# Maxima chunks of an attention step at four places instead of two

## The chip, the cores and the metric

The kernel runs on one core of a Trainium2 chip. The metric is the device time of one launch in microseconds. Matrix products run on TensorE (PE in the profile, its weight loads PEld), reductions and elementwise work on VectorE (DVE), exponentials and copies out of the accumulators on ScalarE (ACT), a few small operations on GpSimd (POOL). SyncE (SP) issues most of the DMAs.

## What is computed

The input is x (16 batches of 256 tokens with 128 channels) and a context of 1601 tokens with 64 channels per batch. Four layers follow each other, each one an attention over the context and a feed-forward part, with residuals and layer norms. What matters here is the attention over the context, with 16 heads. In layers l0, l1 and l3 a head has 8 channels, in l2 it has 32:

```python
scores = jnp.einsum('bhqd,bhkd->bhqk', qh, kh) * scale      # 256 queries x 1601 keys
attn = jax.nn.softmax(scores, axis=-1)
out = jnp.einsum('bhqk,bhkd->bhqd', attn, vh)
```

l0 and l2 have a second attention of x to itself (256 keys), the "own attention" below. Keys, values and feed-forward parts need further matrix products.

## The kernel before

**Slabs and steps.** The attention over the context of one batch and one layer is cut into four slabs of four heads each: 16 batches x 4 layers x 4 = 256 slabs, one after the other. The keys of a head lie on 32 partitions, so the four heads of a slab lie on the four 32-row strips of TensorE. A slab has seven steps (`Slab.steps`, L530): six over two tiles of 128 keys, and a last one over the remaining 65 keys. The scores of a step are transposed: keys on partitions, queries along the free dimension. `st_ops` (L447) computes eight score products (twice as many instructions for l2, whose keys are plain float32) and adds the negated maximum of each query with four further matmuls, the "shift" (st<-nmT,ones). `exps` (L462) takes the exponential on ScalarE, twice per step. `weigh` (L473) multiplies the probabilities with the values into the accumulator `av`, one step later: the values of step j-1 follow the scores of step j (`weigh_back`, L1132).

**Maxima.** The shift of a slab must be known before its first step. It is made during the slab before: `Slab.maxima` (L544) pops one chunk, a matmul of 128 queries of one head with some 400 keys into one bank of the accumulators (bank<-k,q), and a reduction to the maximum on VectorE (mx<-bank, L552). A slab has 2 x 4 x 4 = 32 chunks; the head changes fastest, so neighbouring chunks lie on different strips. When all 32 are done, `Slab.thirds` (L556) reduces them to one negated maximum per query and head (nm, L558) and splits it on POOL into three bfloat16 parts with four operations (L509 to L512); `Slab.shift` (L561) transposes them on TensorE (bank<-ident,nmp) and ScalarE copies the result (nmT).

**Banks.** The pool `pb` (L156) has four banks. They serve the chunks, the accumulator `av` of the slab (held for all its steps), and the products of all other work. The pool `ps` has two buffers for scores, of two banks each.

**Slots.** All other work (layer norms, feed-forward parts, keys, values, own attention, the end of a slab) is written as generators. `slot` (L1073) advances each of them by one piece: first what waits in `later` (the end of a slab, `finish`, L1115), then the line of the keys or of the values in turn, then the chains of the two batches in work and the loading of contexts. A slot can emit much work on TensorE or none. Each step has two slots at its end.

**Order.** The order of the instructions on each engine is the order in which the program emits them; a wait holds up what comes behind it on the same engine. In a step before the change it is: chunks up to `part - 3` (L1173), scores and exponentials (L1176, L1177), three chunks (L1179), values of the step before (L1180), two slots. `part` runs 5, 10, 16, 21, 26, 32, so a step has two or three chunks ahead of the scores and three behind them. `maxima` (L1157) emits the matmuls of one place first and their reductions after them. The last step has no chunks: it begins with `thirds`, and `shift` stands between the values and the slots.

Of the kernel before, what the change touches and what calls it, by code (L numbers as in the profile page):

```python
# [54 lines left out]
def rows_of(kt):  # L55
    return min(P, NK - kt * P)
# [18 lines left out]
def model(ctx: ExitStack, tc: tile.TileContext, d, out):  # L75
# [88 lines left out]
    def bank():  # L164
        return pb.tile([P, 512], F32, tag="bank", name=name("bank"))
# [5 lines left out]
    def mm(o, l, r, start=True, stop=True, free=False):  # L171
        nc.tensor.matmul(out=o, lhsT=l, rhs=r, start=start, stop=stop, skip_group_check=free)  # L172
# [274 lines left out]
    def st_ops(att, s, t0, n, r, nmT, pairs=(0, 1)):  # L447


        sc = {hp: ps.tile([P, 2, 2, T], F32, tag="st", name=name("st")) for hp in pairs}  # L450
        heads = [g for hp in pairs for g in (2 * hp, 2 * hp + 1)]
        for i in range(n):
            k0 = (t0 + i) * P
            for g in heads:
                h = slice(32 * g, 32 * g + 32)
                mm(sc[g // 2][:r, g % 2, i, :], att.k[s][h, k0 : k0 + r], att.q[h, s, :], i == 0, False)
        for g in heads:
            h = slice(32 * g, 32 * g + 32)
            mm(sc[g // 2][:r, g % 2, :n, :], ones16[h, :r], nmT[h, :].unsqueeze(1).broadcast_to([32, n, T]), False, True)
        return [sc[hp] for hp in pairs]  # L460

    def exps(att, sc, n, r):  # L462
        e = probs()
        nc.scalar.activation(e[:r, :, :n, :], sc[:r, :, :n, :], AF.Exp, scale=att.scale)  # L464
        return e

    def zeroed(att):
        a = bank().rearrange("p (u q) -> p u q", u=2)
        n = 1 if att.d8 else 2
        mm(a[:, :n, :], zero16[:, :P], zero16.unsqueeze(1).broadcast_to([1, n, T]), True, False, True)  # L470
        return a

    def weigh(att, s, av, pr, t0, n, r, last, heads=range(4), sums=True, values=True):  # L473
        for i in range(n):
            fin = last and i == n - 1
            if values:
                for g in heads:
                    m = 9 if att.d8 else 32
                    mm(av[32 * g : 32 * g + m, 0, :], att.value(s, t0 + i, g, r), pr[g // 2][:r, g % 2, i, :],
                       False, fin, True)  # L480
            if sums and not att.d8:
                for g in heads:
                    mm(av[32 * g : 32 * g + 32, 1, :], ones[:r, :32], pr[g // 2][:r, g % 2, i, :], False, fin, True)
# [43 lines left out]
    class Slab:  # L527


        steps = [(t, min(2, NT - t), rows_of(t)) for t in range(0, NT, 2)]  # L530
# [13 lines left out]
        def maxima(self):  # L544

            g, q, c, k0, k1 = self.todo.popleft()
            att, s = self.att, self.s
            p = bank()
            h = slice(32 * g, 32 * g + 32)

            def reduce():
                nc.vector.tensor_reduce(self.mx[:, q, g, c : c + 1], p[:, : k1 - k0], AX.X, ALU.max)  # L552

            return lambda: mm(p[:, : k1 - k0], att.q[h, s, q * P : (q + 1) * P], att.k[s][h, k0:k1]), reduce
# [501 lines left out]
    def advance(g):  # L1056
        try:
            return True, next(g)
        except StopIteration:
            return False, None  # L1060

    def begin():

        while began[0] < nb:
            b = began[0]
            n = None if b < LANES else seq.index((b - LANES, "l3"))
            if n is not None and not (n in k_done and n in v_done):
                return
            chains.append([None, load_ctx(b)])
            chains.append([b, life(b)])  # L1070
            began[0] += 1

    def slot():  # L1073
        begin()
        if later:
            g = later.popleft()
            if advance(g)[0]:
                later.appendleft(g)
        for i, l in enumerate(lines):
            if i == turn[0] % 2:  # L1080
                advance(l)
        turn[0] += 1
        for c in list(chains):
            if c[0] is not None and c[0] in ready:
                if not ready[c[0]].done:
                    continue
                del ready[c[0]]
            alive, att = advance(c[1])
            if att is not None:
                ready[c[0]] = att  # L1090
            if not alive:
                chains.remove(c)

    def until(cond):
        for _ in range(2000):
            if cond():
                return
            slot()
        raise RuntimeError("the slots do not come to an end")
# [3 lines left out]
    def slab(i):  # L1103

        n, s = divmod(i, 4)
        if n >= len(seq):
            return None
        b = seq[n][0]
        until(lambda: b in ready and not ready[b].done and n in k_of and s in k_of[n])
        att = ready[b]  # L1110
        att.k, att.v = k_of[n], v_of.setdefault(n, {})
        slabs_of[i] = Slab(att, s, i % 2)
        return slabs_of[i]

    def finish(sl, i):  # L1115

        yield from normalised(sl.att, sl.s, sl.av)
        if sl.s == 3:
            sl.att.done = True
        if not sl.att.d8 or sl.s == 3:  # L1120
            vp_room.give()

    with tc.manual_schedule():
        sl = slab(0)
        while sl.todo:
            for o in sl.maxima():
                o()
        sl.thirds()
        sl.shift()
        back = None  # L1130

        def weigh_back():  # L1132

            nonlocal back
            if back is None:
                return
            sl, i, j, pr = back
            n = i // 4
            t0, m, r = sl.steps[j]
            if j == 0:  # L1140
                until(lambda: (0 if sl.att.d8 else sl.s) in v_of.get(n, {}))
                sl.att.v = v_of[n]
                sl.av = zeroed(sl.att)
            last = j == len(sl.steps) - 1
            weigh(sl.att, sl.s, sl.av, pr, t0, m, r, last)
            back = None
            if last:
                g = finish(sl, i)
                if advance(g)[0]:
                    later.append(g)  # L1150

        for i in range(4 * len(seq)):
            nxt = slab(i + 1)
            steps = sl.steps
            emitted = 0

            def maxima(want):  # L1157

                nonlocal emitted
                ops = []  # L1160
                while nxt is not None and emitted < want:
                    a, c = nxt.maxima()
                    a()
                    ops.append(c)
                    emitted += 1
                for c in ops:
                    c()

            for j, (t0, m, r) in enumerate(steps):

                part = 32 * (j + 1) // (len(steps) - 1)
                if j < len(steps) - 1:
                    maxima(part - 3)  # L1173
                elif nxt is not None:
                    nxt.thirds()
                sc = st_ops(sl.att, sl.s, t0, m, r, sl.nmT)  # L1176
                pr = [exps(sl.att, t, m, r) for t in sc]  # L1177
                if j < len(steps) - 1:
                    maxima(part)  # L1179
                weigh_back()  # L1180
                back = (sl, i, j, pr)
                if j == len(steps) - 1 and nxt is not None:
                    nxt.shift()
                slot()
                slot()
            kp_room.give()
            sl = nxt
        weigh_back()
        until(lambda: not chains and not later)
# [119 lines left out]
```

## Time and profile before

| what | value |
|---|---|
| time, median of 3 runs | 11254.35 us (11251.69 to 11277.46) |
| the profiled execution | 11315.87 us, span 11313.9 us |
| mean granted clock of TensorE | 0.795 |
| ScalarE, exponentials (L464) | 3840, 3500.6 us busy |
| TensorE, values (bank<-p,v) | 2483.3 us busy |
| TensorE, scores (st<-q,k) | 2011.0 us busy |
| TensorE, shift (st<-nmT,ones) | 1291.8 us busy |
| VectorE, nm of a slab (L558) | 256, 186 ns each in the middle |
| DMA, mean busy share of the queue q1 | 11.4% |

A group in the profile is named by the source line of the instruction, its engine and operation, and "what it writes <- what it reads". Nearly all matmuls have the line of one helper, L172, so they are told apart by their tiles. Busy time counts overlapping matmuls of one group once. "Granted clock" is the share of the full clock that TensorE was given in a stretch. A row of the timeline gives start, length, engine, line, operation and tiles, how many instructions are merged in it, and in brackets how long the engine was idle before and for whom it waited.

### The profile page before, as it was taken

The numbers are of one execution on the slowest core, as the hardware profiler recorded it, in microseconds if no ns is written. First come the engines' busy times: TensorE is split into PE (matmuls) and PEld (weight loads), VectorE is DVE, ScalarE is ACT, GpSimd is POOL, SyncE is SP. The second block draws the span as 40 slices with busy tenths as digits, with TensorE's granted clock in tenths as the row PEclk, the third lists the DMA queues.
The fourth block names the chain that finished last, engine by engine and source line by source line (L and its number), as shares of the span: only waits on it lengthen the run. The fifth ranks groups of instructions, "written<-read, shape, count | busy, mean of one in ns | idle before, by whom it ended". The sixth has DMA issues, their size and how long they took to land.

```text
span 11313.9 us, 204909 instructions
## 1 busy us (share of the span) xinstructions
PE 9940.3 (88%) x86834; PEld 5384.7 (48%) x86874; DVE 5942.1 (53%) x13070; ACT 4978.6 (44%) x6812; POOL 952.6 (8%) x2283
## 2 busy tenths in 40 slices
PE   6989899898998979989798897988989989798898
PEld 3445444454444544445454454544544445454454
DVE  4544555445554455545555454554555545455455
ACT  3433454334543445434454344543444434444344
POOL 2000100001000010000100001000010000100000
PEclk7679777796777977789777896778977689777897
DMA  2100111001110011100111001110011100111011
GB/s 57 36 7 15 35 44 36 7 18 36 40 36 7 18 38 39 36 7 18 42 39 31 7 19 42 37 31 7 20 43 36 31 7 19 43 36 32 7 23 26
DMA packets 158827, 313.09 MB, mean 28 GB/s; under 512 B 65163, under 2 KB 116275, under 8 KB 157910
## 3 DMA queue, kind: packets, MB, share of 16 engines
q1 hardware_dynamic: 154676, 297.83, 11.4%
q8 instruction: 683, 11.19, 0.4%
q14 instruction: 234, 1.92, 0.1%
q0 software_dynamic: 768, 1.48, 0.0%
q10 hardware_dynamic: 2466, 0.68, 0.0%
HBM read 98.31 MB, written 2.10 MB: 9 GB/s over the span
## 4 chain that ended last, share of the span: by engine, by line
PE 73%; DVE 13%; ACT 5%; issue 4%; POOL 3%; SPq 2%; DMA 1%; DVEq 0%; POOLq 0%; ACTq 0%
PE bank L172 58%; PE st L172 10%; DVE mx L552 4%; ACT p L464 3%; DVE nm L579 2%; SPq L411 2%; PE mx L172 1%; PE bank L492 1%; PE bank L298 1%; POOL rs L278 1%; DVE z L282 1%; POOL p L603 1%; DVE st L275 1%; DVE hl L405 1%; ACT y L239 1%
## 5 line engine op out<-in xcount | busy, mean ns | idle before, releaser
L552 DVE TENSOR_REDUCE mx<-bank 128x1 f32<-128x400 f32 (+2 forms) x8192 | 4165.5, 568 | 2382.7 <-PE bank L172 2292.8
L464 ACT ACTIVATE p<-st 128x1024 f32<-128x1024 f32 (+1 forms) x3840 | 3500.6, 963 | 3735.0 <-PE st L172 2376.3
L172 PE MATMUL bank<-k,q 32*128 32x400 f32 (+2 forms) x10240 | 3663.6, 574 | 479.6 <-DVE mx L552 265.8
L172 PEld LDWEIGHTS bank<-k,q 32*128 32x128 f32 x10240 | 1653.0, 216 | 1900.6 <-DVE mx L552 1065.7
L172 PE MATMUL bank<-p,v 128*9 128x256 f32 (+3 forms) x27648 | 2483.3, 472 | 32.5 <-POOL p L603 32.5
L172 PE MATMUL st<-q,k 32*128 32x256 f32 (+1 forms) x18176 | 2011.0, 394 | 156.5 <-DVE nm L579 82.4
L172 PEld LDWEIGHTS st<-q,k 32*128 32x128 f32 (+1 forms) x18176 | 1313.4, 213 | 507.4 <-ACT p L464 174.3
L172 PE MATMUL st<-nmT,ones 32*128 32x512 bf16 (+1 forms) x7680 | 1291.8, 442 | 0.0
L172 PEld LDWEIGHTS bank<-p,v 128*9 128x9 f32 (+3 forms) x27648 | 688.0, 105 | 1243.6 <-issue 988.7
L172 PE MATMUL bank<-p,ones 128*32 128x256 f32 (+1 forms) x7680 | 611.3, 392 | 20.2 <-ACT p L464 20.2
L509 POOL CAST nmp<-nm 128x8 bf16<-128x8 f32 x384 | 83.7, 218 | 6017.6 <-DVE nm L558 4434.6
L579 DVE TENSOR_REDUCE nm<-mx 128x4 f32<-128x1024 f32 x256 | 301.7, 1221 | 317.2 <-PE mx L172 312.5
L172 PEld LDWEIGHTS <-ones 32*128 32x128 bf16 (+1 forms) x7680 | 410.2, 109 | 41.1
L278 POOL TENSOR_TENSOR rs<-rs,neghalf 128x2 f32<-128x2 f32 x240 | 167.6, 698 | 3002.5 <-DVE rs L277 3002.5
L239 ACT COPY v<-bank 128x512 f32<-128x512 f32 (+3 forms) x592 | 228.8, 449 | 372.2 <-PE bank L172 372.2
L172 PEld LDWEIGHTS bank<-p,ones 128*32 128x32 f32 (+1 forms) x7680 | 251.8, 113 | 217.2 <-ACT p L464 39.4
L603 POOL TENSOR_SCALAR_AFFINE_SELECT p<-p 128x1024 f32<-128x1024 f32 x256 | 266.6, 1063 | 841.6 <-PE bank L172 524.1
L502 DVE RECIPROCAL rc<-bank 128x256 f32<-128x256 f32 x128 | 224.7, 1756 | 175.4 <-PE bank L172 171.6
L172 PE MATMUL bank<-ws,h 128*128 128x128 f32 x1664 | 307.0, 351 | 3.2 <-DVE h L1027 0.8
L464 ACT ACT_TABLE_LOAD x141 | 180.9, 1283 | 262.0 <-PE st L172 139.1
L172 PEld LDWEIGHTS bank<-ws,h 128*128 128x128 f32 x1664 | 275.7, 255 | 38.6 <-DVE h L1027 12.5
L492 PE MATMUL bank<-ident,y 128*128 128x128 f32 x512 | 136.3, 360 | 155.1 <-ACT y L239 154.6
(240 smaller groups left out, 7258.1 us busy)
## 6 DMA issues: line engine op xcount, KB each, us to landing
k<-hl SPq DMA_DIRECT2D x768, 200.2 KB, 4.0
q<-hl SPq DMA_DIRECT2D x1024, 32.0 KB, 1.9
ws<-in_s_l_a_li_dram SPq DMA_DIRECT2D x32, 768.0 KB, 4.2
ws<-in_s_l3f_dram SPq DMA_DIRECT2D x32, 768.0 KB, 6.7
ws<-in_s_l0f_dram SPq DMA_DIRECT2D x32, 512.0 KB, 5.5
ws<-in_s_l_a_qkv_dram SPq DMA_DIRECT2D x16, 768.0 KB
k<-hl SPq DMA_DIRECT2D x256, 32.0 KB, 1.9
ws<-in_s_l3f_dram SPq DMA_DIRECT2D x16, 384.0 KB
```

What stands on the lines that cost most here:

```text
L172: nc.tensor.matmul(out=o, lhsT=l, rhs=r, start=start, stop=stop, skip_group_check=free)
L239: nc.scalar.copy(o, i)
L275: nc.vector.bn_stats(out=st[:, q, :], in_=src[:, q, :])
L278: nc.gpsimd.tensor_tensor(rs, rs, neghalf[:, 0:2], ALU.pow)
L282: nc.vector.tensor_scalar(z[:, q, :], src[:, q, :], mv[:, q, 0:1], rs[:, q : q + 1], ALU.subtract, ALU.mult)
L411: nc.sync.dma_start(out=raw(o)[r::4, :], in_=raw(hl[c])[32 * s : 32 * s + 32, :])
L464: nc.scalar.activation(e[:r, :, :n, :], sc[:r, :, :n, :], AF.Exp, scale=att.scale)
L492: nc.tensor.transpose(t[:, q * P : (q + 1) * P], y[:, q * P : (q + 1) * P], ident)
L502: nc.vector.reciprocal(rc, av[:, 1, :])
L552: nc.vector.tensor_reduce(self.mx[:, q, g, c : c + 1], p[:, : k1 - k0], AX.X, ALU.max)
L579: nc.vector.tensor_reduce(o, sc[hp], AX.X, ALU.max, negate=True)
L603: nc.gpsimd.affine_select(out=e, in_=e, pattern=[[0, 2], [sign * P, 2], [-sign, T]], compare_op=op, fill=0.0, base=0, channel_multiplier=sign,
```

## The change

The chunks of a step stand at four places instead of two: ahead of the scores, behind the exponentials, behind the values of the step before, and between the two slots. `ends` holds how many chunks of the 32 are to be out at each place; over the six steps with chunks it runs 1, 2, 4, 5 | 6, 8, 9, 10 | 12, 13, 14, 16 | 17, 18, 20, 21 | 22, 24, 25, 26 | 28, 29, 30, 32. So each place has one or two chunks, and a step has five or six as before. In the last step all ends are 0 and no chunk is emitted; `thirds` and `shift` stand where they stood.

```diff
-                part = 32 * (j + 1) // (len(steps) - 1)
-                if j < len(steps) - 1:
-                    maxima(part - 3)
-                elif nxt is not None:
-                    nxt.thirds()
+
+                ends = [32 * (4 * j + k) // (4 * (len(steps) - 1)) for k in range(1, 5)]
+                if j == len(steps) - 1:
+                    ends = [0] * 4
+                    if nxt is not None:
+                        nxt.thirds()
+                maxima(ends[0])
                 sc = st_ops(sl.att, sl.s, t0, m, r, sl.nmT)
                 pr = [exps(sl.att, t, m, r) for t in sc]
-                if j < len(steps) - 1:
-                    maxima(part)
+                maxima(ends[1])
                 weigh_back()
                 back = (sl, i, j, pr)
                 if j == len(steps) - 1 and nxt is not None:
                     nxt.shift()
+                maxima(ends[2])
                 slot()
+                maxima(ends[3])
                 slot()
```

## The prediction

> **What bounds the kernel now.** I read the page first (shares, clock, chain, groups), then the totals of the waits, then the timeline of single steps, then a table by stretches.
>
> ```profile
> PE 9940.3 (88%) x86834; PEld 5384.7 (48%) x86874; DVE 5942.1 (53%) x13070; ACT 4978.6 (44%) x6812; POOL 952.6 (8%) x2283
> ...
> PE 73%; DVE 13%; ACT 5%; issue 4%; POOL 3%; SPq 2%; DMA 1%; DVEq 0%; POOLq 0%; ACTq 0%
> ...
> L552 DVE TENSOR_REDUCE mx<-bank 128x1 f32<-128x400 f32 (+2 forms) x8192 | 4165.5, 568 | 2382.7 <-PE bank L172 2292.8
> ...
> L172 PE MATMUL bank<-k,q 32*128 32x400 f32 (+2 forms) x10240 | 3663.6, 574 | 479.6 <-DVE mx L552 265.8
> ```
>
> TensorE bounds: busy 88% of the span, 73% of the chain, at a mean granted clock of 0.795. The chunks of the maxima (bank<-k,q) alone have it busy for 3663.6 us, beside or without other work. There are 8192 of them, 32 for each of 256 slabs, each with one reduction on VectorE; the 64 slabs of layer l2, with plain f32 keys, need two matmul instructions per chunk (6144 + 2 x 2048 = 10240).
>
> ```profile
> PEld bank L172 <- DVE mx L552: 1282.9, 3016, 5.7
> ...
> PE bank L172 <- DVE mx L552: 265.8, 316, 5.4
> ...
> PE bank L492 <- ACT y L239: 154.6, 201, 2.4
> ```
>
> These are waits: who waited for whom, us in total, how often, longest. A chunk's weight load waits 3016 times for a reduction: it wants one of the four banks, and one is held by av for the whole slab. The wait costs more than TensorE's own 265.8 us of idleness, because chunks that wait come one by one. A step with 8-wide heads shows it:
>
> ```profile
> 3016.14 0.45 PE L172 MATMUL bank<-k,q 32*128 32x402 f32 x2
> ...
> 3016.73 1.45 PE L172 MATMUL bank<-k,q 32*128 32x402 f32 x3
> ...
> 3018.11 1.05 PE L172 MATMUL bank<-p,v 128*9 128x256 f32 x16
> ...
> 3020.15 0.45 PE L172 MATMUL bank<-k,q 32*128 32x400 f32 x2
> ```
>
> Two chunks before the scores start together and run beside them: they use other 32-row strips. Of the three after the scores, the first still fits beside the shift matmuls; the other two wait for banks and stand alone, some 0.48 us each. First chunk to values: 1.97 us.
>
> ```profile
> 3180.47:3185.28 4.81, 4.81 (x40) 2.28 (x36) 2.98 (x6) 1.94 (x2) 0.00 (x0) 0.50 0.00 0
> 3188.48:3191.43 2.95, 2.91 (x37) 1.51 (x33) 2.50 (x6) 2.16 (x3) 0.00 (x0) 1.00 0.00 0
> ```
>
> Two steps whose slots are empty (length, then busy PE, PEld, DVE, ACT, POOL, clock): 4.81 us at clock 0.50 and 2.95 us at 1.00. In the second VectorE is near its limit, 2.50 us for 5 reductions, 0.50 each in a row; it idles 0.45 us while the values run.
>
> [...]
>
> **The change part by part.** Nothing is removed or added in kind: 8192 chunks, 8192 reductions, same operands, no DMA. [...] Now the ends run 1, 2, 4, 5, 6, 8, 9, 10, 12 and so on: four places with 1 or 2, 5.33 per step in both. I went through the matmuls in order of time and counted what stands between two groups of values. Of 869 full 8-wide steps 31% have no slot work on TensorE, 28% up to 1.5 us (I take it as one slot working), 41% more (both); of those with none 44% run at full clock. There are 1152 such steps with chunks and 384 of l2.
>
> *The block around the scores* keeps 2.67 chunks, which need three banks at most and so wait for nothing: 0.9 us for scores and shift with the first chunks, plus 0.2 for a chunk at their tail, 1.1 us instead of 1.97. Saved: 0.87.
>
> *The other 2.67 chunks* stand behind the values and between the slots. Where both slots have matmuls, each place stands alone: one chunk, or two together, 0.45 us (the row at 3020.15), 0.9 in all. So with both slots working this part is worth nothing. With one slot empty a place joins its neighbour: about 0.45 saved, 322 x 0.45 = 145 us. With both empty all 5.33 chunks stand in one row with the scores. At full clock VectorE then limits: 5.33 x 0.50 = 2.67 against some 3.07 (2.95 scaled from 5 to 5.33 chunks is 3.1), 0.4 saved in 44% of 357 steps, 157: 63 us. At half clock (the other 200) the timeline has 1.6 us for scores, shift and three chunks beside them (3180.49 to 3182.08); 2.33 more, spread over four strips at some 0.65 each, add about 0.4; values take 1.83 (3183.45 to 3185.28). With 0.3 for what doesn't fit neatly 4.1 instead of 4.81: 200 x 0.7 = 140 us.
>
> *Waits in slot steps.* The idleness right before chunks is 479.6 us (page), nearly all of it for reductions and for the slots' own evacuations. A chunk that comes alone finds a free bank more often. Bounds 0 and 480; I take half, 240.
>
> *Layer l2.* A lone chunk is two passes, 0.93 us in the timeline at 991.61, some 0.85 of it for itself. Its block (timeline at 991.61 to 995.06) is 3.45 us, with five chunks, of which about two lie beside scores; the other three alone account for some 1.65, so with 2.67 chunks it would be 1.8. Saved 1.65, given back 1.7 with both slots working, 0.85 with one, 0.45 with none; with shares of 37, 45 and 18% about 0.55 x 384 = 210 us.
>
> *Behind the values at a slab's end* the finish copies y on ScalarE and the next slot transposes it; TensorE idles 154.6 us for it. A slab's first step now puts two chunks into exactly that hole: 0.45 of the 0.7 us. I take 100.
>
> *What is late next.* VectorE works through its instructions in program order. Reductions of place three now stand ahead of slot one's VectorE work, those of place four ahead of slot two's; TensorE waits for these results a slot later (L298 for z, 151.7 us idle in the totals of the waits). Also each slot finds one or two banks more in use. Bounds[...]: 0 to 0.6 us in some 900 steps, 540; I take 330. POOL and SP are passed by nothing: chunks issue no DMA and no POOL work, and the slots issue theirs in the same order.
>
> *The end of a slab* is the one wait that the change lengthens by design:
>
> ```profile
> 3194.93 0.19 DVE L558 TENSOR_REDUCE nm<-mx 128x8 f32<-128x32 f32 x1
> ...
> 3196.40 0.29 PE L172 MATMUL bank<-ident,nmp 128*128 128x128 bf16 x2
> ```
>
> nm needs all 32 reductions, then four POOL operations (3195.25 to 3196.35), then the shift, which TensorE reaches 1.5 us after the last scores begin (3194.86). Before, the last chunks were ahead of a group of values and this just fitted. Now chunks 31 and 32 stand between the slots. With slot two empty (70% of last steps had no slot work before them) they end 0.45 us after the place, their reductions 0.2 + 1.1 later, nm 0.19, and 1.25 to the shift: 3.15 us, a stall of 1.65. Where VectorE limits the slab anyway nothing is lost. Bounds 0 to 0.7 x 256 x 1.65 = 295; I take half, 145.
>
> Sum: 145 + 63 + 140 + 240 + 210 + 100 - 330 - 145 = 423 us. The profiled execution took 11315.87 us (span 11313.9), 0.5% above the median of 11254.35. 10893 of 11316 is 0.963, times the median: **10834 us**.
>
> **The rivals.**
> *A, even trade*: the lone places give back what the lone chunks after the scores took (0.9 against 0.87), in most steps, and slot waits eat the rest. For it: both slots work in 41% of steps. Against it: 31% have none. Without the terms of empty slots (348) and half of l2 (105), with the other terms kept: 423 - 453, about no change; with half of these left, about 200 us gained, 11,060.
> *B, slower*: the end of the slab decides. If the stall of 1.65 us comes in every slab (255 x 1.65 = 420) and the block around the scores gains 250 us in all, the time is 11254 + 170 = 11,424. It decides once the other gains are under 0.27 us per step (420 / 1536). Against it: slot work covers it in 30%, VectorE-bound slabs do not feel it.
> *C, the clock follows*: [...] a step that flips takes 2.7 to 3. If the 200 cold empty steps flip (another 1.2 each) the time is 10834 - 240, about 10,590. Against it: which activity flips the clock no view shows.
> That the change does nothing is excluded: the order on TensorE and VectorE does change.
>
> **How the numbers follow.** Forecast 0.50 (its own range 10,680 to 11,000), A 0.18, B 0.14, C 0.18. The range is 10,480 to 11,240: it takes in C with some more flips and A to its dear end, and leaves out B and a small rest. A measurement of this kernel can tell about 0.3% from no change. Faster: 0.50 + 0.18 + four fifths of A, 0.82; same 0.05; slower 0.13.
>
> **What would show it.** VectorE's releases of bank<-k,q weight loads fall well below 3016; idleness before chunks falls from 479.6 us; TensorE's idleness for y falls from 154.6; idleness for POOL's nmp (75.9 us in the totals of the waits) rises by 100 to 300. Full-clock empty steps near 2.7 us, half-clock ones near 4.1 or gone. It is wrong if idleness before chunks stays (banks held by slots, not by the clump), or if the rise at nmp exceeds 400 us.

## The result, and the profile after

The changed kernel takes 11857.25 us (median of 4 runs, 11845.16 to 11870.78); the kernel before takes 11265.9 us beside it. The ratio is 1.0522, interval 1.0495 to 1.0548: slower by 5%, where 3.7% faster was forecast. The profiled execution has a span of 11861.8 us against 11313.9, at a mean granted clock of 0.787 against 0.795.

First the page of the changed kernel, shares and costliest groups:

```profile
PE 9990.1 (84%) x86834; PEld 5346.9 (45%) x86874; DVE 6086.6 (51%) x13070; ACT 4979.8 (42%) x6812; POOL 957.0 (8%) x2283
...
PE 69%; DVE 16%; ACT 5%; issue 4%; POOL 3%; SPq 2%; DMA 1%; POOLq 0%; DVEq 0%; ACTq 0%
...
L552 DVE TENSOR_REDUCE mx<-bank 128x1 f32<-128x400 f32 (+2 forms) x8192 | 4348.6, 570 | 3754.7 <-PE bank L172 3701.4
...
L172 PE MATMUL bank<-k,q 32*128 32x400 f32 (+2 forms) x10240 | 3850.8, 579 | 529.2 <-DVE mx L552 323.9
```

TensorE is busy 50 us more, within a span that is 548 us longer. So some 500 of the 548 us are idleness. The reductions wait 3701 us for chunks (2293 before). That is no cost in itself: it says that VectorE is not what limits. The idleness right before chunks did not fall but rose, from 479.6 to 529.2 us. Then the totals of the waits:

```profile
PEld bank L172 <- DVE mx L552: 1228.5, 1875, 3.5
...
PE bank L172 <- DVE mx L552: 406.2, 651, 3.2
...
PE bank L172 <- POOL nmp L512: 276.0, 224, 3.6
...
PE bank L492 <- ACT y L239: 220.4, 185, 2.5
```

Weight loads wait for a reduction 1875 times instead of 3016, but longer each (0.66 us on average, 0.43 before). TensorE's own waits grew in all three of the other rows: for reductions from 265.8 to 406.2 (82 us of it ahead of other products than chunks, by the 323.9 in the page), for the shift (nmp) from 75.9 to 276.0, for y from 154.6 to 220.4. The row of nmp in the kernel before:

```profile
PE bank L172 <- POOL nmp L512: 75.9, 55, 5.3
```

Chunks aside, TensorE's instructions are the same in both kernels. So I left the chunks out of both traces, went through the other matmuls in order of time, and summed by how much each moved the latest end on. That gives the time from one kind of work to the next, whatever chunks stand between. The table is my count from the traces, in us:

| from -> to | before | after | behind_values (below) |
|---|---|---|---|
| scores -> values | 2178 | 963 | 1773 |
| values -> scores (no slot work) | 257 | 757 | 271 |
| values -> slot work | 750 | 1731 | 1578 |
| slot work -> slot work | 2790 | 3192 | 2943 |
| slot work -> scores | 1045 | 912 | 570 |
| within scores | 1826 | 2030 | 1547 |

From scores to values 1215 us were gained, and 204 lost again within the scores. Behind the values more was lost: 500 us to the next scores, 981 to slot work, 402 from slot work to slot work.

A second count cuts the traces at the reduction nm, of which each slab has one, and sorts the slabs by their own layer and that of the next slab, whose chunks they carry. In us, for the profiled executions:

| slabs | before | after | no_front | start_only | y_on_dve | behind_values |
|---|---|---|---|---|---|---|
| 183 8-wide, next 8-wide | 7423 | 7549 | 7421 | 7387 | 7143 | 6944 |
| 56 of l2, next of l2 | 2883 | 3311 | 3080 | 3065 | 3211 | 3065 |
| all the rest | 1008 | 1001 | 941 | 964 | 985 | 971 |

The last four columns are experiments below. For the noise of the rows: before_y_dve, which takes the same time as the kernel before, differs from it by +48, -24 and -87 us. So 429 of the 548 us are lost in the 56 slabs of l2, for which the prediction had a gain. By the same count the mean granted clock in them fell from 0.950 to 0.881 (weighted by time, 0.940 to 0.879); in the 8-wide slabs it stayed (0.748 and 0.744).

Three places of the changed kernel's timeline show how chunks hold up the rest. First a step without slot work:

```profile
3354.36 0.70 PE L172 MATMUL bank<-k,q 32*128 32x402 f32 x3
3355.10 2.02 DVE L552 TENSOR_REDUCE mx<-bank 128x1 f32<-128x402 f32 x4 [1.80 <-PE bank L172]
3355.73 0.70 PE L172 MATMUL bank<-k,q 32*128 32x400 f32 x1 [0.66 <-DVE mx L552]
3355.73 0.91 PE L172 MATMUL st<-q,k 32*128 32x256 f32 x7
```

The two places behind the values and the one ahead of the next scores have joined to a row of four chunks. Three start at once. The fourth has no bank until the first reduction is done, and the scores, behind it in order, wait with it: they begin 1.37 us after the row's start instead of beside it. The whole step, by the table by stretches:

```profile
3354.36:3359.15 4.79, 4.13 (x39) 1.99 (x36) 3.08 (x6) 2.03 (x3) 0.00 (x0) 0.50 0.00 0
```

4.79 us, where the like step before took 4.81 and 4.1 was forecast. Then the end of the same slab:

```profile
3363.85 0.70 PE L172 MATMUL bank<-k,q 32*128 32x400 f32 x3
...
3364.91 1.34 PE L172 MATMUL bank<-p,v 128*9 128x256 f32 x16
...
3366.15 0.19 DVE L558 TENSOR_REDUCE nm<-mx 128x8 f32<-128x32 f32 x1
...
3367.63 0.28 PE L172 MATMUL bank<-ident,nmp 128*128 128x128 bf16 x2 [1.39 <-POOL nmp L512]
```

The last three chunks stand right ahead of the last scores; nm comes after the values have begun, and the shift is 1.39 us late. Last the start of the next slab:

```profile
3368.87 1.94 ACT L464 ACTIVATE p<-st 128x1024 f32<-128x1024 f32 x2 [0.54 <-PE st L172]
...
3369.84 0.70 PE L172 MATMUL bank<-k,q 32*128 32x402 f32 x2
...
3370.69 0.38 ACT L239 COPY y<-bank 128x256 f32<-128x256 f32 x1
...
3371.12 0.69 PE L492 MATMUL bank<-ident,y 128*128 128x128 f32 x2 [0.59 <-ACT y L239]
```

The copy of y stands behind both exponentials of the first step on ScalarE. So TensorE's wait for y runs from the scores, not from the values: 1.94 + 0.38 us, and the two chunks behind the values don't shorten it.

### The profile page after: what moved, and what is told of

Its sections match the earlier page's. It is cut to its first block, busy times and chain, and to the rows that moved or that the text cites. A ratio compares the mean times of both kernels' runs of the same rounds, so it can differ in the third digit from the quotient of the medians.

```text
span 11861.8 us, 204934 instructions
## 1 busy us (share of the span) xinstructions
PE 9990.1 (84%) x86834; PEld 5346.9 (45%) x86874; DVE 6086.6 (51%) x13070; ACT 4979.8 (42%) x6812; POOL 957.0 (8%) x2283
## 4 chain that ended last, share of the span: by engine, by line
PE 69%; DVE 16%; ACT 5%; issue 4%; POOL 3%; SPq 2%; DMA 1%; POOLq 0%; DVEq 0%; ACTq 0%
PE bank L172 55%; PE st L172 11%; DVE mx L552 8%; ACT p L464 3%; DVE nm L579 2%; SPq L411 2%; PE mx L172 1%; PE bank L492 1%; DVE rc L502 1%; PE bank L298 1%; DVE hl L405 1%; DVE z L282 1%; POOL nmp L512 0%; DVE st L275 0%; ACT y L239 0%
## 5 line engine op out<-in xcount | busy, mean ns | idle before, releaser
L552 DVE TENSOR_REDUCE mx<-bank 128x1 f32<-128x400 f32 (+2 forms) x8192 | 4348.6, 570 | 3754.7 <-PE bank L172 3701.4
L172 PE MATMUL bank<-k,q 32*128 32x400 f32 (+2 forms) x10240 | 3850.8, 579 | 529.2 <-DVE mx L552 323.9
L172 PEld LDWEIGHTS bank<-k,q 32*128 32x128 f32 x10240 | 1547.4, 219 | 2253.2 <-DVE mx L552 1099.6
L172 PE MATMUL bank<-p,v 128*9 128x256 f32 (+3 forms) x27648 | 2441.3, 465 | 3.0 <-POOL p L603 2.1
L172 PE MATMUL st<-q,k 32*128 32x256 f32 (+1 forms) x18176 | 2178.1, 411 | 213.0 <-ACT p L464 124.5
L172 PEld LDWEIGHTS st<-q,k 32*128 32x128 f32 (+1 forms) x18176 | 1413.5, 218 | 506.8 <-ACT p L464 219.0
L172 PE MATMUL st<-nmT,ones 32*128 32x512 bf16 (+1 forms) x7680 | 1408.7, 454 | 0.0
L239 ACT COPY v<-bank 128x512 f32<-128x512 f32 (+3 forms) x592 | 229.1, 449 | 630.1 <-PE bank L172 630.1
L172 PE MATMUL bank<-ident,nmp 128*128 128x128 bf16 x768 | 106.4, 242 | 290.4 <-POOL nmp L512 276.0
L492 PE MATMUL bank<-ident,y 128*128 128x128 f32 x512 | 145.9, 382 | 220.4 <-ACT y L239 220.4
L239 ACT CAST nmT<-bank 128x256 bf16<-128x256 f32 (+1 forms) x320 | 130.5, 415 | 434.7 <-PE bank L172 434.5
```

Source lines behind the costliest of these rows:

```text
L239: nc.scalar.copy(o, i)
L492: nc.tensor.transpose(t[:, q * P : (q + 1) * P], y[:, q * P : (q + 1) * P], ident)
```

## The experiments

Each kernel but before_y_dve has the numbers of chunks in a table instead of the formula, a row for each of the six steps with chunks, a column for each place; the loop is that of the change. The medians of the kernel before beside them were 11268 to 11291 us. In the first four kernels (no_front to behind_values) the source lines are 8 higher than in the others, so L552 is L560 there.

**Nothing ahead of the scores (no_front).**

```diff
-(1, 2, 4, 5), (6, 8, 9, 10), (12, 13, 14, 16), ... (28, 29, 30, 32)
+(0, 2, 4, 5), (5, 8, 9, 10), (10, 13, 14, 16), ... (26, 29, 30, 32)
```

> The change with the chunks of its first place (ahead of the scores) moved to the second (behind them): places with 0, 2 or 3, 1 or 2, 1 or 2 chunks. With empty slots no more than 3 chunks stand in a row ahead of the scores. Theory R (a row of four chunks with three free banks holds up the scores): most of the 500 us between values and the next scores come back, 11,300 to 11,450, and the time between values and scores in steps without slot work falls to that of before. Theory L (chunks that stand alone beside slot work cost more than they save): places three and four are unchanged, so 11,750 or more.

11468.41 us, ratio 1.0168 (1.0120 to 1.0217). Two thirds of the loss are gone, and the time from values to scores is 303 us (757 in the change). That speaks for the row of four, and against the cost of lone chunks as the main loss. The 389 us are a net sum: scores to values went back from 963 to 1650 us. The wait for the shift did not fall; it was 330.9 us.

**The slab's maxima end early (early_end).**

```diff
-(28, 29, 30, 32)
+(29, 32, 32, 32)
```

> The change, but in the last step with chunks all of them stand ahead of and behind the scores (3 and 3, as before the change), so that the maxima of a slab end as early as before. Theory E (the end of the slab): the 290 us of idleness before the transposes of nmp fall to about 85 and the time falls by 150 to 250, to about 11,650. If the end of the slab merely takes a wait that would be paid elsewhere: no more than 50 us.

11653.97 us, ratio 1.0318 (1.0269 to 1.0366). As forecast by theory E; the row in the totals of the waits is now

```profile
PE bank L180 <- POOL nmp L520: 83.7, 63, 6.1
```

against 276.0. Undoing the late end alone is worth some 200 us.

**No place between the slots (no_between).**

```diff
-(1, 2, 4, 5), (6, 8, 9, 10), (12, 13, 14, 16), ...
+(1, 3, 5, 5), (6, 9, 10, 10), (12, 15, 16, 16), ...
```

> The change without its fourth place; the chunks from between the slots stand behind the scores: 1 or 2, 2 or 3, 1 or 2, 0. With empty slots at most 3 or 4 in a row ahead of the scores, mostly 3. Theory R: 11,350 to 11,500. Theory L: half of the lone chunks remain, about half of the loss, 11,550.

11681.5 us, ratio 1.0331 (1.0275 to 1.0388). Worse than both theories said. Values to scores came back (272 us), but most of the gain from scores to values went with it (1888 us). So the row of four is not all.

**Chunks from ahead of the scores behind the values (behind_values).**

```diff
-(2, 5), (7, 10), (13, 16), (18, 21), (23, 26), (29, 32)                                  # before: ahead, behind the scores
+(2, 5, 7, 7), (7, 10, 13, 13), (13, 16, 18, 18), (18, 21, 23, 23), (23, 26, 29, 29), (29, 32, 32, 32)
```

> The kernel before, with the two or three chunks from ahead of the scores moved back behind the values, ahead of the slots; the three behind the scores stay. With empty slots the order of instructions is that of before. Only steps with slot work differ: the chunks there stand alone instead of beside the scores. Theory L: 0.4 us in each of some 1060 such steps, 11,550 to 11,700. Theory R: no row is longer than before, so within 1% of before, 11,250 to 11,370.

10994.12 us, ratio 0.9743 (0.9698 to 0.9788). Neither theory said that: it is 2.6% faster than the kernel before. The page and, below it, the waits:

```profile
PE 9512.8 (87%) x86834; PEld 5129.8 (47%) x86874; DVE 5957.4 (54%) x13070; ACT 4986.7 (45%) x6812; POOL 956.4 (9%) x2283
...
L180 PE MATMUL bank<-k,q 32*128 32x400 f32 (+2 forms) x10240 | 2963.4, 552 | 293.0 <-DVE mx L560 184.4
```

```profile
PE bank L500 <- ACT y L247: 54.3, 146, 1.8
```

Chunks have TensorE busy for 2963 us instead of 3664, and idle before them for 293 instead of 480. They now stand ahead of the slots' work, when banks are free, and not behind it, when the slots hold them: slot work to scores takes 570 us (1045 before). By slabs the gain is all in the 8-wide layers (7423 to 6944 us); l2 is still slower than before (2883 to 3065). This order for the 8-wide layers alone was not tried. And with the banks empty at the scores, the three behind them run together. Its timeline in a step with slot work:

```profile
3027.45 0.51 PE L180 MATMUL st<-q,k 32*128 32x256 f32 x8
3027.79 0.39 PE L180 MATMUL st<-nmT,ones 32*128 32x512 bf16 x4
3027.84 0.70 PE L180 MATMUL bank<-k,q 32*128 32x402 f32 x3
...
3028.47 1.05 PE L180 MATMUL bank<-p,v 128*9 128x256 f32 x16
```

Scores to values in 1.0 us with three chunks, where the step shown before took 1.97 with five. A chunk alone behind the values is thus cheaper than theory L took it to be.

**Both edits (no_front_early)**, with the last row of early_end in no_front.

> The change with both edits at once: nothing ahead of the scores (as in no_front, 11468 us), and in the last step with chunks three ahead of and three behind the scores (as in early_end). If the row of four and the end of the slab are separate losses that add, idleness before nmp falls from 331 to under 110 us and the time by 200 to 260 from no_front, to about 11,240. If they are one loss seen twice: no better than 11,400.

11399.06 us, ratio 1.0098 (1.0071 to 1.0125): 69 us below no_front, neither 200 nor nothing. The wait for nmp fell to 78.8 us, but three chunks ahead of the last scores join the place between the slots to a row of four or five again: values to scores rose from 303 to 486 us. The two edits overlap.

**And the first step as before (no_front_early_start).**

```diff
-(0, 2, 4, 5), (5, 8, 9, 10), ...
+(2, 5, 5, 5), (5, 8, 9, 10), ...
```

> As no_front_early, but the first step of a slab has two chunks ahead of and three behind the scores, as before the change, and none at the other two places. Theory S (the start of a slab: ScalarE's two exponentials of the first step stand ahead of the copy of y, and chunks around the scores are what fills that time): idleness before the transposes of y stays near or below 150 us, and the time is 50 to 150 below no_front_early. If the chunks behind the values fill the time just as well: equal within 30 us or worse.

11179.55 us, ratio 0.9923 (0.9897 to 0.9948): 220 us less, more than forecast. By my count from values to the transposes of y 243 us instead of 400. The idleness for y itself did not fall (143.0 to 164.3 us). What changed is where the slab's first chunks stand: two behind the first scores and two behind the values before, five around the scores and none behind the values now. TensorE waits as long for y as before, but has done the slab's first five chunks by then.

**That edit alone on the change (start_only).**

> The change, with only the first step of a slab as before (two chunks ahead of, three behind the scores, none at the other places). Theory S: as from no_front_early to no_front_early_start, 150 to 220 us below the change, 11,640 to 11,710. If the gain there was a gift of the other two edits: within 60 us of the change.

11420.05 us, ratio 1.0108 (1.0081 to 1.0135): 437 us below the change, twice what theory S said, so of the three edits taken singly that of the slab's start brings most. Values to scores did not change (748 us), so it is not the row of four once more. But by slabs only 162 us of the gain are in the 183 8-wide slabs, and 246 in the 56 of l2, where no y is copied. There VectorE takes the reciprocal and the product of a slab's end straight from `av` (L502, L503), and products of the next slots wait for it. In the change that is

```profile
PE bank L172 <- DVE oT L503: 77.7, 64, 2.1
```

and 8.5 us in start_only; the kernel before has no such row. The rows of start_only in the totals of the waits: the shift as late as in the change, y as before it.

```profile
PE bank L172 <- POOL nmp L512: 286.8, 224, 3.4
...
PE bank L492 <- ACT y L239: 147.6, 201, 2.4
```

**y copied by VectorE (y_on_dve).** The places are those of the change.

```diff
-            evac(y, av[:, 0, :])
+            nc.vector.tensor_copy(y, av[:, 0, :])
```

> The change, with y copied by VectorE instead of ScalarE. Theory S says that TensorE waits for y because the copy stands behind two exponentials on ScalarE (2 us): the 220 us of idleness before the transposes of y fall below 90, and the time by 80 to 200 from 11,857. If the copy itself or the chunks are the cause: idleness stays, time within 50 us or longer (VectorE has the reductions).

11379.36 us, ratio 1.0070 (1.0048 to 1.0092): 478 us below the change. The wait is gone:

```profile
PE bank L492 <- DVE y L488: 30.1, 121, 0.8
```

By my count 213 us come from the path to y itself; the rest is spread over all other work, at a mean clock of 0.829 instead of 0.787. By slabs 406 us are gained in the 8-wide ones, and 100 in those of l2, which copy no y; the wait for oT stays (81.5 us).

**The control: the kernel before with y on VectorE (before_y_dve).**

> The kernel before with y copied by VectorE, the control for y_on_dve. Theory S (the change made TensorE's wait for y longer: 155 us idle before, 220 after): part of the 480 us that y_on_dve gained is here too, but less, 100 to 250 us, 11,040 to 11,190. If the wait for y costs both kernels the same and is not a loss of the change: the same 450 or more, 10,840 or less.

11264.93 us, ratio 1.0002 (0.9987 to 1.0016): nothing, against both expectations. Its idleness for y stayed too:

```profile
PE bank L492 <- DVE y L488: 142.1, 200, 0.9
```

VectorE's copy stands behind the reductions of the five chunks there (five in a row take 2.51 us at 3016.62 of the kernel before), as ScalarE's stood behind the exponentials (1.94 us). So the control does not show the copy fully hidden in the order before; it shows that moving it to VectorE is worth nothing there. The 478 us belong to the order of the change. That start_only gains a like sum, 437 us, doesn't make it the same loss: most of that is in l2, and most of the 478 us is not.

**All three losses undone (no_front_early_y_dve).**

> no_front_early (11399 us: the row of four and the end of the slab undone) with y copied by VectorE. If the three losses are the whole of it and they add: 11,000 to 11,150, below the kernel before by as much as the shorter block around the scores brings. If they overlap: 11,250 or more.

11119.99 us, ratio 0.9874 (0.9836 to 0.9913), inside the range for "the three are the whole". With none ahead of the scores except in the last step with chunks, no late end and a wait for y of 64.8 us, the order is 1.3% faster than before. The wait for oT at the start of l2's slabs is still there (66.5 us).

**One chunk more behind the values (behind_balanced)**: 3 behind the values in all steps but the last, 2 behind the scores in three of the six.

> behind_values (10994 us) with one more chunk behind the values and one less behind the scores in most steps (2 behind the scores, 3 behind the values). Theory: each chunk behind the scores beyond the first waits alone for a bank, some 0.48 us; three behind the values still find three banks. 100 to 250 us below behind_values, about 10,830. If chunks behind the values cost as much: 10,990 within 60.

11165.17 us, ratio 0.9905 (0.9875 to 0.9934). A miss: 170 us slower than behind_values. Scores to values fell by 122 us, values to slot work rose by 386.

**Between the slots instead (between_only).**

```diff
-(2, 5, 7, 7), (7, 10, 13, 13), (13, 16, 18, 18), ...
+(2, 5, 5, 7), (7, 10, 10, 13), (13, 16, 16, 18), ...
```

> behind_values with the two or three chunks behind the values moved on to between the two slots. With empty slots the same order of instructions. If the place between the slots is as good as the one behind the values: 10,994 within 60. Theory: the place behind the values is the better one, since there the chunks fill TensorE's wait for y (54 us idle in behind_values, 155 before the change), which the first slot begins with: idleness for y back at 150 or more, 11,080 to 11,200.

11309.48 us, ratio 1.0022 (1.0004 to 1.0039), 315 us slower than behind_values. Idleness for y is back at 151.5 us, as theory had it, but the time is longer than it said. Two groups of products in the slots (w_l_Wcv and w_l_a_wkv by ctxT) take some 300 us more by my count, but others take as much less. What is left of the loss is spread: slot work to scores 167 us, within the scores 129, scores to values 122, at a mean clock of 0.803 instead of 0.836. What causes it stays open.

**A fourth chunk behind the values (behind_four).**

```diff
-(2, 5, 8, 8), (8, 10, 13, 13), (13, 15, 18, 18), ...     # behind_balanced
+(2, 4, 8, 8), (8, 9, 13, 13), (13, 14, 18, 18), ...
```

> behind_balanced (11165 us) with four chunks behind the values and one or two behind the scores. Theory R (a fourth chunk in a row waits for a bank, with everything behind it): the time from values to scores in steps without slot work, 257 us before the change and within 20 us of it in behind_values and behind_balanced, rises to 650 or more, and the time to 11,300 or more. If the length of the row does not matter: under 350 us there, and about 11,200.

12146.49 us, ratio 1.0753 (1.0727 to 1.0779): a jump of 980 us for one chunk more in the row, at a mean clock of 0.781 instead of 0.837. Values to scores: 277 us with three in the row, 769 with four. In the steps with slot work the fourth holds up the slots: values to slot work 2524 us instead of 1964. Its timeline has the change's picture again:

```profile
3202.45 0.70 PE L172 MATMUL bank<-k,q 32*128 32x400 f32 x3
3203.19 2.02 DVE L552 TENSOR_REDUCE mx<-bank 128x1 f32<-128x400 f32 x4 [1.39 <-PE bank L172]
3203.82 0.70 PE L172 MATMUL bank<-k,q 32*128 32x400 f32 x1 [0.66 <-DVE mx L552]
```

**A fourth chunk behind the scores (behind_more)**: 4 behind the scores, 1 or 2 behind the values.

> behind_values (10994 us) with one more chunk behind the scores and one fewer behind the values (4 and 1 or 2). If the more the better, as behind_balanced against behind_values suggests: 10,900 or less. If three is the best number because of three free banks: 11,050 or more.

12243.66 us, ratio 1.0848 (1.0815 to 1.0882). The fourth chunk holds up the values. It can wait long, as VectorE may have slot work ahead of the reductions:

```profile
3209.44 0.70 PE L172 MATMUL bank<-k,q 32*128 32x400 f32 x1
...
3211.90 2.00 DVE L552 TENSOR_REDUCE mx<-bank 128x1 f32<-128x400 f32 x4
3212.51 0.70 PE L172 MATMUL bank<-k,q 32*128 32x400 f32 x1 [2.38 <-DVE mx L552]
```

**The fastest order with y on VectorE (behind_values_y_dve).**

> behind_values (10994 us) with y copied by VectorE. There the chunks behind the values already fill the wait (54 us idle): theory S says little is left, 10,900 to 11,010. If the copy matters for another reason (the bank of av comes free sooner, ScalarE is relieved): 10,700 or less.

11017.87 us, ratio 0.9787 (0.9751 to 0.9823): a little above the range of theory S, and not to be told from behind_values, as the intervals overlap. On top of that order the edit to the copy brings nothing.

## Why the prediction was wrong

The prediction had 423 us of gain, and 591 us were lost. Its terms in turn, with what the runs put in their place:

**The block around the scores: right for the 8-wide layers.** 0.87 us were forecast for each of 1152 steps. By my count the mean time from the first score to the first value fell from 2.46 to 1.41 us.

**Layer l2: the term that was off by most.** Forecast was a gain of 210 us: 1.65 saved around the scores in each of 384 steps, two thirds of it given back. From the first score to the first value an l2 step fell from 2.86 to 2.32 us only, 0.54 instead of 1.65. And more was given back than the prediction reckoned from the lone chunks' own time: in the 56 slabs values to slot work rose by 320 us, slot work to slot work by 170, values to scores by 95. In sum these slabs lost 429 us. The three losses below occur there too: no_front, early_end and start_only give back 232, 134 and 246 of the 429 us, no_front_early_start 362. At the slab's start the wait is for VectorE's work on `av` (oT, 77.7 us in the change), which the prediction does not name. How much of the 429 us comes through the clock (0.950 to 0.881, and 0.92 to 0.93 with each of the three edits) stays open.

**"All 5.33 chunks stand in one row with the scores": the mechanism that failed.** It took the strips for the only limit and counted banks for the block around the scores alone. Behind the values three places join: one or two chunks from place three, one or two from place four, one or two of the next step's place one. In five of six steps that makes four, and three banks are free. The prediction reckoned 203 us of gain for the 8-wide steps without slot work. The 318 such steps in the trace gained 64 (1323 to 1259 us): what they won from scores to values, 360 us, they lost from values to scores, 371. At full clock they took 3.3 us (3.2 before) and at half clock 4.9 (5.1 before), where 2.7 and 4.1 were forecast. The steps of l2 without slot work lost 82 us. no_front, where the row is three at most, has values to scores back at 303 us, and behind_four and behind_more show the step from three to four: 980 us more than behind_balanced and 1250 more than behind_values, each at a lower clock too.

**The start of a slab: wrong sign.** "A slab's first step now puts two chunks into exactly that hole", 100 us of gain. The hole begins at the scores, because the copy of y waits for ScalarE's two exponentials (1.94 us), and the five chunks that filled it before were cut to two ahead of the values. The two behind them do not make up for it. y_on_dve, which takes that wait away, gains 478 us, 406 of them in 8-wide slabs; start_only gains 437, of which 246 are in the 56 slabs of l2. The control shows that the edit of y_on_dve is worth nothing in the order before. I had read the row "PE bank L492 <- ACT y L239" as a wait for the copy, without asking what stands ahead of the copy on ScalarE.

**The end of a slab: right.** 145 us were taken from bounds of 0 and 295; the wait for nmp rose by 200, and early_end gives 203 us back. Rival B named it, but as the thing that decides; it is the smallest of the three losses.

**Waits before chunks: wrong.** 240 us of gain were forecast; they rose by 50, which the prediction had named as a sign that it is wrong. What held a chunk up here was how many stood in its row and what the slots held, not whether it came alone: the idleness before chunks was 529.2 us in the change and 293.0 in behind_values.

**The cost of the lone chunks** (zero net with both slots working, and 330 us for what is late next): no run measures these terms alone. behind_values shows that the place behind the values can pay, between_only that the place between the slots did not.

**Rival C, the clock:** of the 318 8-wide steps without slot work 126 ran at full clock before and 168 after, as the rival had it, but l2 lost clock, and the mean fell (0.795 to 0.787). With the faster orders it rose (0.836 in behind_values). How much of a difference comes through the clock and how much through the waits themselves no run separates. The three losses do not add: undone singly (no_front, early_end, start_only) they are worth 389, 203 and 437 us, more than the whole of 591.

## What to carry to other kernels

Count buffers along the order that remains when everything optional between two places is empty: places that are apart in the code are neighbours there, and here the first chunk without a bank held up the scores behind it (1.37 us at 3354.36 of the change). Before moving filler away from a wait, follow the awaited instruction back on its own engine; the wait may begin earlier than where it shows, as here for y, by the 1.94 us of the two exponentials. Put work that needs buffers ahead of the work that holds them for long; here that was worth 2.6% (behind_values). And cut a trace by the kinds of its steps before and after: the totals of all layers hid here that most of the loss was in one of them.

## What was not expected of the hardware

One chunk more in a row, over the three free banks, and one fewer behind the scores in return, cost 9% of the whole time (behind_balanced 11165.17 to behind_four 12146.49 us). Removing idleness returned more than its own length: y_on_dve took about 190 us of idleness for y away and gained 478 us, with the mean granted clock up from 0.787 to 0.829; in the kernel before, the same edit moved neither (11264.93 us, clock 0.801). And in the kernel before TensorE was granted half the clock (0.50) all the time from 6350.5 to 6388.0 us, while it was busy 36.6 of these 37.5 us. What sets the clock no run shows.
